# A two-layer graph kernel: block sums transposed by VectorE instead of TensorE, blocks of 480 columns, the input loaded between pieces of the adjacency

## The chip, the core and the metric

The kernel runs on one core of a Trainium2 chip. The metric is the device time of the whole program in microseconds (us), the median of several executions; lower is better. Engines are named as in the profile: PE is TensorE (matrix products), PEld its weight loads, DVE is VectorE, ACT is ScalarE, POOL is GpSimd, SP is SyncE, which here only issues DMA transfers.

## The reference

The inputs are `x` (3327 x 128) and a 0/1 matrix `adj` (3327 x 3327), all in fp32. Two layers follow each other, each of the form x + layer(relu(layernorm(x))):

```
# layer 0
h   = relu(layernorm(x))
deg = adj.sum(axis=1);  deg = 1 where deg == 0
agg = adj.T @ h / deg
y   = agg @ W_n.T + b_n + h @ W_c.T + b_c
x   = x + relu(batchnorm(y) * gamma + beta)
# layer 1: n = 3327, d = 128, h = 8
z = relu(layernorm(x))
q, k, v = (z @ W.T).reshape(128, n, 8)          # for Wq, Wk, Wv
a = einsum('dnh,dmh->dnm', q, k) / sqrt(128) + adj + adj
out = einsum('dnm,dmh->dnh', softmax(a, axis=2), v)
x = x + out.reshape(n, 1024) @ Wo.T
```

Nearly all the work is in the second layer: for each of 128 slices d, a 3327 x 3327 matrix of scores with an inner dimension of only 8, its exponential, and a product with v, which has 8 columns.

## The kernel before

**Layer 0.** The rows of the adjacency come in 26 chunks of 128 rows (tile `a`, 1.66 MB each, three buffers, issued by SP at L431). For each chunk, PE makes seven products (L433) that add up adj.T @ h in seven PSUM banks, ACT sums the rows (L437), and DVE takes a maximum (L440). PE needs `A` = relu(layernorm(x)) for that. In the kernel before, `x` is loaded into `xs` by two large and two small DMAs issued from ACT (L326, L328), and after them ACT issues the ten loads of weights and vectors (L331 to L337). Then seven rounds of `stats` (DVE statistics, ACT square root) and `normalise` (two small DVE operations, four ACT activations) make all of `A`, before the loop over chunks is recorded. `beside` puts transposes and small products of the same layer between chunks.

**Layer 1.** 32 groups (`NG`) of four slices d (`G`) follow each other. In a group the 3328 padded query columns are cut into seven blocks of `QB` columns (before: six of 476 and one of 472), and each block takes 13 steps (`SU`), in each of which two chunks of 128 keys are used. So there are 224 blocks and 2912 steps. The order of all engines is written by hand (manual schedule), in this one loop:

- `product` (L750): two products on PE give scores `s` of 128 keys x 2 x w queries in PSUM (three buffers, two banks each). There are four products in a step.
- For two or three of the four (`plain`), DVE adds the adjacency (`add`, L862) and writes to `d`; one step later a single ACT instruction takes the exponential of all of `d` (`late`, L907).
- For the others (`rest`; one in a step, two in the steps 3, 7 and 11, named `DOUBLE`), ACT takes the exponential straight from PSUM (L871), and POOL multiplies by weights exp(2 adj) that were stored earlier (L874, tile `wt`).
- `second` (L623): PE multiplies the exponentials by v and adds up over the 13 steps, three steps behind (`LAG`). The result of a block, in one bank `av`, holds for each of the four slices (partitions 32b to 32b+8) nine rows: eight sums and the sum that divides them. Two banks `av` alternate between blocks.
- `finish` divides a finished block and stores it. It is a generator; `step()` runs it on, one part each time, in the steps of the next block that `PARTS` lists (step 7 is served at another place of the loop, after the first `add`). In the kernel before the parts are: step 3, DVE copies `av` to `avs` in SBUF (L633); steps 5 and 6, two products each with the identity on PE (L640), which write the transposed sums back into `av`, with the query columns on partitions; step 7, three DVE operations (L648 to L651) divide; step 8, SP issues one DMA to `att` (L658; at the end of a group a second small one, L665).
- `begin` and `go_on` put parts of the next group's projections (L208) and of the last group's output product (L269, L279) into steps 7, 8, 11 and 12; they use the bank `av` of the block that has just been finished.
- `fetch` issues the loads of `at` (adjacency, L738, four buffers) and `wt` (L734, three buffers) two steps ahead, on SP. The loads of the next group's q, k and v are spread over the steps, and POOL sorts k (L192).

The function `attention_shifted` is for other inputs and isn't run here; it calls `finish` too.

Of the kernel before, what the change touches and what calls it, by code (L numbers as in the profile page):

```python
# [9 lines left out]
F32 = mybir.dt.float32  # L10
F32R = mybir.dt.float32r
I32 = mybir.dt.int32
AF = mybir.ActivationFunctionType
ALU = mybir.AluOpType
# [4 lines left out]
N = 3327  # L19
D = 128  # L20
H = 8
P = 128
NC = 26
T = N * D
NP = NC * P
NB = 512
QB = 476
G = 4
EPS = 1e-5
HALF = 0.5 / math.sqrt(D)  # L30
# [3 lines left out]
CH = 4 * NP // D  # L34
NG = D // G
DOUBLE = (3, 7, 11)
PARTS = (3, 5, 6, 7, 8)

def pieces(r):

    return [(p0, p1) for p0, p1 in ((0, r // 16 * 16), (r // 16 * 16, r)) if p1 > p0]
# [3 lines left out]
def tile_two_layer_gnn(  # L47
# [17 lines left out]
    nc = tc.nc  # L65
# [5 lines left out]

    qblocks = [(n0, min(QB, NP - n0)) for n0 in range(0, NP, QB)]

# [13 lines left out]
    att = dram.tile([TP, H], F32, name="att")  # L87
# [8 lines left out]
    attb = att[:T].rearrange("(d n) h -> d n h", n=N)  # L96
    atr = att.rearrange("(n u) h -> n (u h)", u=D)

    ident = const.tile([P, P], F32, name="ident")
# [8 lines left out]
    eps = const.tile([P, 1], F32, name="eps")  # L108
    nc.vector.memset(eps, EPS)
    wqk = [const.tile([P, H * D], F32, name=n) for n in ("wq", "wk", "wv")]  # L110
    wo = const.tile([P, H, D], F32, name="wo")
# [189 lines left out]
    with tc.tile_pool(name="l0", bufs=1) as l0, tc.tile_pool(  # L301
        name="l0adj", bufs=3
    ) as ap, tc.tile_pool(name="l0s", bufs=2) as sp, tc.tile_pool(
        name="l0last", bufs=1
# [3 lines left out]
        xs = ll.tile([P, NC, D], F32, name="xs")  # L308
        A = l0.tile([P, NC, D], F32, name="A")
# [6 lines left out]
        wn = l0.tile([P, D], F32, name="wn")  # L316
        wc = l0.tile([P, D], F32, name="wc")
        cols = l0.tile([P, 4], F32, name="cols")
        bias = l0.tile([P, 1], F32, name="bias")
# [2 lines left out]

        xr = x[: (NC - 1) * P, :].rearrange("(c p) d -> p c d", p=P)
        nc.vector.memset(xs[:, NC - 1, :], 0.0)
        for c0, c1 in ((0, 8), (8, NC - 1)):
            nc.scalar.dma_start(xs[:, c0:c1, :], xr[:, c0:c1, :])  # L326
        for p0, p1 in pieces(N - (NC - 1) * P):
            nc.scalar.dma_start(  # L328
                xs[p0:p1, NC - 1, :], x[(NC - 1) * P + p0 : (NC - 1) * P + p1, :]
            )  # L330
        nc.scalar.dma_start(wc, WcT)  # L331
        for i, b in enumerate((b_n, b_c, gamma, beta)):
            nc.scalar.dma_start(cols[:, i : i + 1], b.rearrange("o d -> d o"))
        nc.scalar.dma_start(wn, WnT)
        for t, w in zip(wqk, (WqT, WkT, WvT)):
            nc.scalar.dma_start(t, w)
        nc.scalar.dma_start(wo, WoT.rearrange("(e p) o -> p e o", p=P))  # L337

        st = l0.tile([P, NC, 6], F32, name="ln_st")
        mv = l0.tile([P, NC, 2], F32, name="ln_mv")  # L340
# [4 lines left out]
        def stats(i, root=True):  # L345
            cs = range(4 * i, min(NC, 4 * i + 4))
            for c in cs:
                nc.vector.bn_stats(st[:, c, :], xs[:, c, :])
            for c in cs:
                nc.vector.bn_aggr(mv[:, c, :], st[:, c, :])  # L350
            if root:
                roots(4 * i, min(NC, 4 * i + 4))

        def roots(c0, c1):
            nc.scalar.activation(sd[:, c0:c1], mv[:, c0:c1, 1], AF.Sqrt, bias=eps)
# [7 lines left out]
        def normalise(i, dst):  # L363

            factors(4 * i, min(NC, 4 * i + 4))
            for c in range(4 * i, min(NC, 4 * i + 4)):
                nc.scalar.activation(  # L367
                    dst[:, c, :], xs[:, c, :], AF.Relu,
                    bias=mr[:, c : c + 1], scale=rs[:, c : c + 1],
                )  # L370
# [7 lines left out]
            return pt[:, :n, :], slice(4 * i, 4 * i + n)  # L378

        NQ = (NC + 3) // 4  # L380
        stats(0)
        for i in range(NQ):
            if i + 1 < NQ:
                stats(i + 1)
            normalise(i, A)
        nc.vector.tensor_add(bias, cols[:, 0:1], cols[:, 1:2])

        def beside(x):

            if x < NQ:  # L390
                pt, cs = turned(x, A, aside)
                nc.scalar.copy(B[:, cs, :], pt)
            elif x < 2 * NQ:
                n0 = (x - NQ) * NB
                w = min(NB, NP - n0)
                nc.tensor.matmul(
                    aside[:, :w], wc, B2[:, n0 : n0 + w], start=True, stop=True
                )
                nc.scalar.activation(
                    C2[:, n0 : n0 + w], aside[:, :w], AF.Identity, bias=bias  # L400
                )
            elif x < 2 * NQ + 4:
                i = x - 2 * NQ
                sq = sp.tile([P, NB], F32, name="sq")
                w = wqk[i // 2][:, i % 2 * NB : (i % 2 + 1) * NB]
                nc.gpsimd.tensor_tensor(sq, w, w, ALU.mult)  # L406
                nc.tensor.matmul(aside[:1, :], ones[:, :1], sq, start=True, stop=True)  # L407
                nc.vector.tensor_reduce(norm[:, i : i + 1], aside[:1, :], AX.X, ALU.max)
# [20 lines left out]
        for c in range(NC):  # L429
            a = ap.tile([P, 7 * NB], F32, name="a")  # L430
            nc.sync.dma_start(a[:, :N], adj[c * P : (c + 1) * P, :])  # L431
            for i, (n0, w) in enumerate(blocks):
                nc.tensor.matmul(  # L433
                    acc[i][:, :w], A[:, c, :], a[:, n0 : n0 + w],
                    start=(c == 0), stop=(c == NC - 1),
                )
            nc.scalar.activation(  # L437
                junk, a[:, :N], AF.Copy, accum_out=deg[:, c : c + 1]
            )
            nc.vector.tensor_reduce(  # L440
                amax[:, c : c + 1], a[:, :N], AX.X, ALU.max, apply_absolute_value=True
            )
            if c >= 1:
                beside(c - 1)

            i = c - 2 * NQ - 5
            if 0 <= i < NQ - 2 and 4 * i + 4 <= c:
                spread(i)
# [17 lines left out]
        b = l0.tile([1, 6], F32, name="bound")  # L466
# [118 lines left out]
        q, k, v = sets[0]  # L585
# [41 lines left out]

    def finish(rp, av, d0, n0, w):

        J = 4  # L630
        R = -(-w // J)
        avs = rp.tile([P, QB], F32, name="avs")
        nc.vector.tensor_copy(avs[:, : R * J], av[:, : R * J])  # L633
        yield

        pt = av[:, : J * G * (H + 1)].rearrange("p (j q) -> p j q", j=J)

        some = ident.rearrange("p (b h) -> p b h", h=32)[:, :, : H + 1]
        for j in range(J):
            nc.tensor.matmul(  # L640
                pt[:R, j, :], avs[:, j : j + (R - 1) * J + 1 : J], some, start=True, stop=True
            )
            if j % 2:
                yield
        pv = pt.rearrange("p j (b h) -> p b j h", h=H + 1)
        ri = rp.tile([P, G, J], F32, name="ri")

        nc.vector.tensor_scalar(ri[:R], pv[:R, :, :, H], 1e-30, None, ALU.max)  # L648
        nc.vector.reciprocal(ri[:R], ri[:R])
        o = rp.tile([P, G, J, H], F32, name="oq")  # L650
        nc.vector.tensor_tensor(  # L651
            o[:R], pv[:R, :, :, :H], ri[:R].unsqueeze(3).to_broadcast([R, G, J, H]),
            ALU.mult,
        )
        yield

        r, j = divmod(min(w, N - n0), J)
        nc.sync.dma_start(  # L658
            attb[bass.ds(d0, G), n0 : n0 + r * J, :].rearrange(
                "b (p j) h -> p b (j h)", j=J  # L660
            ),
            o[:r].rearrange("p b j h -> p b (j h)"),
        )
        if j:
            nc.sync.dma_start(  # L665
                attb[bass.ds(d0, G), n0 + r * J : n0 + r * J + j, :].rearrange(
                    "b (o j) h -> o b (j h)", o=1
                ),
                o[r : r + 1, :, :j, :].rearrange("p b j h -> p b (j h)"),
            )  # L670

    def rows_of(c):
        return min(P, N - c * P)

    def attention():


        with tc.tile_pool(name="adj", bufs=4) as ap, tc.tile_pool(
# [13 lines left out]
            if True:  # L692
# [35 lines left out]
                def fetch(x):  # L728
                    while wanted and wanted[0][0] <= x:
                        _, kind, i, y, c = wanted.pop(0)  # L730
                        n0, w = qblocks[y]
                        if kind:
                            a = wp.tile([P, QB], F32, name="wt")
                            nc.sync.dma_start(a[:, :w], wd[c - WC, :, n0 : n0 + w])  # L734
                        else:
                            a = ap.tile([P, 2, QB], F32, name="at")
                            n = min(2, WC - 2 * c)
# [25 lines left out]
                def more_weights(i, y, s):  # L763
# [13 lines left out]
                    if phase == 0:  # L777
                        have["w"] = wk.tile([P, 2, QB], F32, name="t4")
                        nc.sync.dma_start(
# [59 lines left out]
                for x, (i, y, s) in enumerate(steps):  # L839
# [15 lines left out]
                    plain, rest = pairs(s)  # L855
                    d = ep.tile([P, 3, 2, QB], F32, name="d")
                    es = [d[:, j] for j in range(len(plain))]
# [36 lines left out]
                    else:  # L894
                        add(2, product(i, y, *plain[2]))
                    if s in PARTS and s != DOUBLE[1]:
                        step()
# [219 lines left out]
```

## Time and profile before

| what | value |
|---|---|
| median of 3 runs | 10377.37 us (10372.69 to 10381.02) |
| the profiled execution: its time, its span | 10381.98 us, 10380.2 us |
| mean granted TensorE clock in it | 0.992 |
| busy: PE, ACT, DVE, POOL | 9995.3, 9923.2, 9366.9, 8439.0 us |
| layer 0, until the first scores | 0 to 261.7 us |
| layer 1 | the rest, some 10100 us |
| L862, DVE add of 128 x 952 | 1.14 us |
| L871, ACT exponential of 128 x 952; L907, of 128 x 2856 | 0.97 us; 2.6 us |
| L633, DVE copy of a block's sums | 0.65 us, 224 times |
| L640, PE products with the identity | four entries of one part: 1.06 us, 448 parts |

Durations of single instructions run until their results are written, and instructions of one engine overlap at their ends, so that ten of them in a row take less than ten durations. A matmul of fp32 has two entries in the trace. "Idle before" is the time in which an engine had nothing running ahead of an instruction, with what ended that wait.

### The profile page before, as it was taken

What the parts mean: (1) busy time and instruction counts of PE and PEld (TensorE: products, weight loads), DVE (VectorE), ACT (ScalarE), POOL (GpSimd) and SP (SyncE); (2) the same over time, 40 slices, a digit from 0 to 9 for tenths busy, and PEclk for the clock granted to TensorE, in tenths of its full rate; (3) what the DMA queues carried; (4) which work ended last, traced back from release to release, by engine and by line L of the source; (5) the groups of instructions that cost most, each with busy time, mean ns of one, the idle gap of its engine ahead of it and who ended that gap; (6) DMA issues with size and microseconds to landing.
All of it is one profiled execution on the core that took longest, in us unless ns stands there. A gap on an engine that the chain in (4) does not pass through costs nothing. (4 is left out here: it accounts for less than half of the span.)

```text
span 10380.2 us, 189900 instructions
## 1 busy us (share of the span) xinstructions
PE 9995.3 (96%) x73327; PEld 3082.3 (30%) x73327; DVE 9366.9 (90%) x9533; ACT 9923.2 (96%) x6655; POOL 8439.0 (81%) x4317
## 2 busy tenths in 40 slices
PE   7899999999999999999999999999999999999999
PEld 3222222222222222222222222222222222222222
DVE  5789999999999999999999999999999999999998
ACT  4899999999999999999999999999999999999998
POOL 1678888888888888888888888888888888888887
PEclk9899999999999999999999999999999999999999
DMA  6766666666666666666665666666666665666554
GB/s 228 221 177 164 163 170 167 166 165 165 163 166 170 165 165 162 164 168 167 167 164 159 168 167 168 167 161 162 167 169 167 167 161 159 171 169 167 157 153 127
DMA packets 1114449, 1735.99 MB, mean 167 GB/s; under 512 B 194622, under 2 KB 1089980, under 8 KB 1105852
## 3 DMA queue, kind: packets, MB, share of 16 engines
q1 hardware_dynamic: 1108766, 1716.94, 60.9%
q8 instruction: 575, 9.42, 0.4%
q10 hardware_dynamic: 4350, 4.20, 0.1%
q14 instruction: 342, 2.80, 0.1%
q0 software_dynamic: 416, 2.63, 0.1%
HBM read 1621.05 MB, written 102.38 MB: 166 GB/s over the span
## 5 line engine op out<-in xcount | busy, mean ns | idle before, releaser
L862 DVE SCALAR_TENSOR_TENSOR d<-at,s 128x952 f32<-128x952 f32 x8064 | 8797.4, 1141 | 681.7 <-PE s L750 397.6
L874 POOL TENSOR_TENSOR f<-f,wt 128x952 f32<-128x952 f32 (+1 forms) x3584 | 7939.0, 2233 | 1674.3 <-ACT f L871 1649.9
L907 ACT ACTIVATE d<-d 128x2856 f32<-128x2856 f32 (+1 forms) x2912 | 7027.9, 2413 | 2.2 <-DVE d L862 1.9
L623 PE MATMUL av<-d,v 128*9 128x476 f32 x32256 | 5065.6, 566 | 0.7 <-ACT d L907 0.7
L750 PE MATMUL s<-q,k 32*128 32x476 f32 x23296 | 4087.3, 475 | 313.8 <-ACT f L871 243.5
L871 ACT ACTIVATE f<-s 128x952 f32<-128x952 f32 (+1 forms) x3584 | 3396.9, 970 | 281.8 <-PE s L750 266.0
L750 PEld LDWEIGHTS s<-q,k 32*128 32x128 f32 x23296 | 1739.5, 182 | 5500.2 <-DVE d L862 3005.9
L623 PE MATMUL av<-f,v 128*9 128x476 f32 x14336 | 2849.0, 566 | 0.0
L623 PEld LDWEIGHTS av<-d,v 128*9 128x9 f32 x32256 | 583.3, 88 | 1161.5 <-issue 1149.6
L640 PE MATMUL av<-ident,avs 128*119 128x36 f32 (+1 forms) x1792 | 474.1, 391 | 0.8 <-DVE avs L633 0.8
L640 PEld LDWEIGHTS av<-ident,avs 128*119 128x119 f32 (+1 forms) x1792 | 422.9, 308 | 103.1 <-issue 101.5
L623 PEld LDWEIGHTS av<-f,v 128*9 128x9 f32 x14336 | 316.6, 88 | 112.4 <-issue 88.7
L192 POOL CAST k<-ks 128x256 fp32r<-128x256 f32 x434 | 283.8, 654 | 0.0
L433 PE MATMUL acc<-a,A 128*128 128x512 f32 (+1 forms) x364 | 151.6, 569 | 24.2 <-ACT A L367 23.4
L238 POOL TENSOR_TENSOR o<-pf,o 104x512 fp32r<-104x512 f32 x124 | 160.0, 1291 | 9.9
L633 DVE COPY avs<-av 128x476 f32<-128x476 f32 (+1 forms) x224 | 145.4, 649 | 4.6 <-PE av L623 4.6
L440 DVE TENSOR_REDUCE amax<-a 128x1 f32<-128x3327 f32 x26 | 93.7, 3611 | 36.4 <-DMA a<-in_adj 36.4
L433 PEld LDWEIGHTS acc<-a,A 128*128 128x128 f32 x364 | 69.0, 192 | 109.0 <-issue 84.5
L236 DVE TENSOR_SCALAR pf<-av,low_half 104x512 f32<-104x512 f32 x62 | 46.6, 751 | 46.8 <-PE av L208 46.6
L406 POOL TENSOR_TENSOR sq<-wk 128x512 f32<-128x512 f32 x2 | 2.1, 1042 | 102.5 <-PE aside L407 102.5
L234 DVE COPY pf<-av 104x512 f32<-104x512 f32 x62 | 42.9, 692 | 46.9 <-PE av L208 46.9
L437 ACT ACTIVATE junk<-a 128x3327 bf16<-128x3327 f32 x26 | 77.5, 2979 | 7.1 <-DMA a<-in_adj 6.8
(123 smaller groups left out, 1032.3 us busy)
## 6 DMA issues: line engine op xcount, KB each, us to landing
at<-in_adjT SPq DMA_DIRECT2D x1728, 476.0 KB
wt<-wd SPq DMA_DIRECT2D x1536, 238.0 KB
at<-in_adjT SPq DMA_DIRECT2D x288, 472.0 KB
wt<-wd SPq DMA_DIRECT2D x256, 236.0 KB
ks<-kT SPq DMA_DIRECT2D x496, 104.0 KB
q<-qT SPq DMA_DIRECT2D x496, 104.0 KB
a<-in_adj SPq DMA_DIRECT2D x26, 1663.5 KB
kT<-o SPq DMA_DIRECT2D x128, 208.0 KB
```

Source lines behind the costliest of these rows:

```text
L192: nc.gpsimd.tensor_copy(k[:, c : c + n, half * 64 : half * 64 + 64], ks.bitcast(F32).rearrange("g (p c) -> g c p", c=NC)[:, c : c + n, :],)
L238: nc.gpsimd.tensor_tensor(o[:CH, 1], f[:CH], o[:CH, 0].bitcast(F32), ALU.subtract)
L433: nc.tensor.matmul(acc[i][:, :w], A[:, c, :], a[:, n0 : n0 + w], start=(c == 0), stop=(c == NC - 1),)
L440: nc.vector.tensor_reduce(amax[:, c : c + 1], a[:, :N], AX.X, ALU.max, apply_absolute_value=True)
L623: nc.tensor.matmul(av[32 * b : 32 * b + H + 1, :w], tiles[2][:, b, c, :], e, start=first, stop=last,)
L633: nc.vector.tensor_copy(avs[:, : R * J], av[:, : R * J])
L640: nc.tensor.matmul(pt[:R, j, :], avs[:, j : j + (R - 1) * J + 1 : J], some, start=True, stop=True)
L750: nc.tensor.matmul(p[:, x, :we], k[rs, c, :], q[rs, n0 : n0 + we], start=True, stop=True,)
L862: nc.vector.scalar_tensor_tensor(d[:, j, :, :w], have[0, i, y, c // 2][:, c % 2, :w] .unsqueeze(1).to_broadcast([P, 2, w]), SAFE / 2, p[:, ...
L871: nc.scalar.activation(f[:, :, :w], p[:, :, :w], AF.Exp, scale=2.0)
L874: nc.gpsimd.tensor_tensor(f[:, :, :w], f[:, :, :w], have[1, i, y, c][:, :w].unsqueeze(1).to_broadcast([P, 2, w]), ALU.mult,)
L907: nc.scalar.activation(flat, flat, AF.Exp, scale=2.0)
```

## The change

There are three edits.

1. `finish` no longer uses PE. DVE transposes the block's sums in squares of 32 x 32 (`nc.vector.transpose`), from `av` in PSUM to `avs` in SBUF. The columns of `av` are read with a stride of J (15, in the last block 14), so that a partition gets J neighbouring queries. The division then reads SBUF. The result goes out in four DMAs of 32 partitions, one for each slice (in the last block of a group eight, as the last query is padding). The parts now stand in steps 3, 7 and 8.
2. Blocks have 480 columns instead of 476: six of 480 and one of 448. All are multiples of 32. There are still seven blocks in a group.
3. `x` is loaded by SP, its first four chunks ahead of the adjacency, the rest behind its first and second chunk. `stats` and `normalise` run inside the loop over chunks. Weights and vectors are loaded by POOL instead of ACT. A first square root of a constant is put ahead on ACT.

```diff
-QB = 476
+QB = 480
-PARTS = (3, 5, 6, 7, 8)
+PARTS = (3, 7, 8)
...
-        for c0, c1 in ((0, 8), (8, NC - 1)):
-            nc.scalar.dma_start(xs[:, c0:c1, :], xr[:, c0:c1, :])
...
+        nc.sync.dma_start(xs[:, :4, :], xr[:, :4, :])
+        def load_x(c):
+            if c < 2:
+                c0, c1 = ((4, 12), (12, NC - 1))[c]
+                nc.sync.dma_start(xs[:, c0:c1, :], xr[:, c0:c1, :])
...
+        root = l0.tile([P, 1], F32, name="root")
+        nc.scalar.activation(root, eps, AF.Sqrt)
+        for t, w in zip(wqk, (WqT, WkT, WvT)):
+            nc.gpsimd.dma_start(t, w)
+        nc.gpsimd.dma_start(wc, WcT)
...
-        stats(0)
-        for i in range(NQ):
-            if i + 1 < NQ:
-                stats(i + 1)
-            normalise(i, A)
...
             nc.sync.dma_start(a[:, :N], adj[c * P : (c + 1) * P, :])
+            load_x(c)
+            if c < NQ:
+                if c == 0:
+                    stats(c)
+                normalise(c, A)
+                if c + 1 < NQ:
+                    stats(c + 1)
...
     def finish(rp, av, d0, n0, w):
-        J = 4
-        R = -(-w // J)
-        avs = rp.tile([P, QB], F32, name="avs")
-        nc.vector.tensor_copy(avs[:, : R * J], av[:, : R * J])
+        J = -(-w // 32)
+        avs = rp.tile([P, QB // 32, 32], F32, name="avs")
+        nc.vector.transpose(
+            avs[:, :J, :].rearrange("p j h -> p (j h)"),
+            av[:, : 32 * J].rearrange("p (q j) -> p j q", j=J),
+        )
         yield
-        pt = av[:, : J * G * (H + 1)].rearrange("p (j q) -> p j q", j=J)
-        some = ident.rearrange("p (b h) -> p b h", h=32)[:, :, : H + 1]
-        for j in range(J):
-            nc.tensor.matmul(
-                pt[:R, j, :], avs[:, j : j + (R - 1) * J + 1 : J], some, start=True, stop=True
-            )
-            if j % 2:
-                yield
...
+        nc.vector.tensor_scalar(ri[:, :J], avs[:, :J, H], 1e-30, None, ALU.max)
+        nc.vector.reciprocal(ri[:, :J], ri[:, :J])
...
+        r = 32 - (n0 + 32 * J > N)
+        for b in range(G):
...
+            nc.sync.dma_start(ab[:r], ob[:r])
+            if r < 32:
+                nc.sync.dma_start(ab[r:, : (J - 1) * H], ob[r:, : (J - 1) * H])
```

## The prediction

> **What bounds the kernel now.** I read the page's busy shares first, then the stretch table, to see whether the share is even over the run.
>
> ```profile
> PE 9995.3 (96%) x73327; PEld 3082.3 (30%) x73327; DVE 9366.9 (90%) x9533; ACT 9923.2 (96%) x6655; POOL 8439.0 (81%) x4317
> ...
> 2000.00:4000.00 2000.00, 1948.57 (x14557) 596.04 (x14553) 1841.95 (x1856) 1951.31 (x1298) 1680.73 (x855) 1.00 0.62 166
> ```
>
> The columns of the second line are the stretch, its length, busy time of PE, PEld, DVE, ACT and POOL, granted clock, DMA share and GB/s. PE and ACT both look full (97.5%), but the timelines tell them apart. First ACT over three steps of a block, then PE over the same time; the bracket is the idle time before an instruction and what ended it.
>
> ```profile
> 5005.22 2.64 ACT L907 ACTIVATE d<-d 128x2832 f32<-128x2832 f32 x1
> 5008.48 0.96 ACT L871 ACTIVATE f<-s 128x944 f32<-128x944 f32 x1 [0.62 <-PE s L750]
> 5009.33 2.56 ACT L907 ACTIVATE d<-d 128x2832 f32<-128x2832 f32 x1
> 5012.37 0.96 ACT L871 ACTIVATE f<-s 128x944 f32<-128x944 f32 x1 [0.48 <-PE s L750]
> ```
>
> ```profile
> 5005.58 0.49 PE L750 MATMUL s<-q,k 32*128 32x472 f32 x4
> 5005.99 1.06 PE L640 MATMUL av<-ident,avs 128*119 128x36 f32 x4
> 5006.99 0.57 PE L623 MATMUL av<-d,v 128*9 128x472 f32 x2
> ...
> 5009.90 1.06 PE L640 MATMUL av<-ident,avs 128*119 128x36 f32 x4
> ```
>
> ACT works without a hole except behind the two L640 parts, which keep PE from the next scores. In the 400 us from 4600 on, all ACT's waits are such pairs (0.59 to 0.62 and 0.47 to 0.49 us), one pair a block; blocks start 44.74 us apart (4606.19 to 4650.93). From 5015.7 on, steps without L640 follow at 3.29 to 3.35 us with ACT never idle. So ACT sets the pace, and L640 costs it 1.1 us a block. The groups of 1000 to 9000 us confirm the sum:
>
> ```profile
> L871 ACT ACTIVATE f<-s 128x952 f32<-128x952 f32 (+1 forms) x2863 | 2712.4, 970 | 193.8 <-PE s L750 181.3 <-POOL k L192 12.5
> L907 ACT ACTIVATE d<-d 128x2856 f32<-128x2856 f32 (+3 forms) x2327 | 5615.7, 2413 | 0.2
> ```
>
> 193.8 us over 179.5 blocks is 1.08 us a block. (The share put down to POOL's sorting is one member of a pair, at 4833.53 us with 0.48 us, so it is the same wait under another name.)
>
> **The change part by part.** *L640 leaves.* ACT's 1.08 us a block, times 224 blocks, is 242 us. Counting L640's own busy time (474 us) would be too much: part of it is time that PE has to spare, as between 5015 and 5019 PE itself waits. Nothing above 242 us is to be had in steady state, since ACT is then full. The first group runs at a granted clock of 0.77 to 1.00 with ACT only 77 to 97% busy (300 to 660 us), where the delays may be longer; at most another 1 us for each of its 7 blocks, kept for the range.
>
> *The transpose takes the copy's place on DVE, in step 3.* The trace has no such instruction. The nearest row is the copy it replaces: same engine, same source in PSUM, 128 x 476 in 0.65 us. The far rows, by pace per element: POOL's product, 2.23 us for 952, would give 1.13 us for 480; DVE's reciprocal, slowest of all, takes 0.25 us for 16 elements against 0.17 for the scaling of the same 16, so 5.3 ns more for each, on the copy's 1.35 ns: 3.2 us. Below the copy's 0.65 us I see no reason for it to fall, since it reads as many elements. I take 0.7 us. What hides it: step 3 has only two adds, 2 x 1.09 us (13 adds in a row take 14.22 us), in a step of some 3.36 us, so 1.18 us are free; a step of three adds leaves 0.09. Up to about 1.2 us the transpose costs nothing; each further us goes into ACT's wait. Queued behind it on DVE are the adds of step 4, on which L907 and the score buffers wait.
>
> *The division in step 7* keeps its three operations (0.17 + 0.25 + 0.29 us) and reads about as many elements, 15, 15 and 120 instead of 16, 16 and 128. It frees the bank `av` no longer, the transpose does that four steps earlier: PE's waits on L651 before the projections (72.6 us over the run) go, but as ACT shows no wait there, I count nothing. DVE, 920 us busy in 1000, has 41.1 us in a block and keeps a block of 43.7 us to 94%.
>
> *Four DMAs on SP instead of one, in step 8*: 3 x 0.33 us more, with the wait for L651 in front of them as now. Behind them stands the next `at`. In the trace that one is issued at 5014.65 and is for the step two further on than the engines' next, some 7 us ahead, and lands in 3.5 us. Hidden; if not, 1 us a block. The packets fall from 476 of 128 B to 128 of 480 B.
>
> *Blocks of 480.* Columns, instructions and steps stay as many as before: nothing. *The end*: 1.9 us of L640 at 10358.8 go, three to seven more issues of 0.33 us come: nothing.
>
> *Layer 0.* PE's first product waits until 23.45 us, because ACT stands in two small loads:
>
> ```profile
> 2.31 12.04 ACTq L328 DMA_DIRECT2D xs<-in_x  x2
> ...
> 20.86 1.28 ACT L355 ACT_TABLE_LOAD   x1 [19.46 <-DMA cols<-in_beta]
> ```
>
> Now 256 KB of `x` lead SP's queue. With 155 GB/s up to 4 us and 428 after, they are in at about 4 us; statistics, root, factors and one activation (0.9 + 0.4 + 0.3 + 0.35 + 0.4) make the first `A` at 6.5; the first chunk lands at about 8. Then data rules: up to the third chunk 6.6 MB, with POOL's 2.2 MB of weights at 0.4 MB per us they take until some 24 us, and the fourth chunk starts at 24 + 6.6 = 30.6 us. Before, it started near 43.2. From there PE sets the pace as before (seven products of two entries in some 6 us; inside the loop ACT has about 5.6 us and DVE 5.2 a chunk, both less). Gain: 12 us; bounds 16 (the start at 8) and 0 (all lost again to loads).
>
> *Sum*: 10381.98 - 242 - 12 = 10128 us for an execution like the profiled one, which is 4.6 us above the median. On the median: **10123 us**.
>
> **A rule against it.** Row first: the granted clock is 1.00 in all stretches from 1000 to 10000 us, and in steps without L640 too (1.00 in 5019.00 to 5022.30 and 5022.30 to 5025.65). The Trainium skill ("TensorE: Matmul & The Clock Gate", Part 1) says that the array falls to half its clock after an idle window of some 3.4 us, which speaks against taking work from PE. By the rule a block without L640 would be in danger only if PE paused that long; the trace's waits of PE in these steps are under 0.7 us, so both give the same sum here.
>
> The same skill ("VectorE: DVE Perf Modes", The three transpose paths) has 311 ns for 128 columns on VectorE; my estimate from it, 3.75 times as much, is 1.17 us for 480, and the sum would still be as above. No run here shows it yet.
>
> **The rivals.** *Half the gain comes back (a second wait).* DVE goes to 94% and POOL to 86%; the adds or POOL's products are then late in some steps. For it: DVE already makes PE wait for L862 often. Against it: steps 7 and 11, where DVE has the division, a projection copy of 0.69 to 0.75 us and a wait of 0.6 to 0.85 us on top, show no ACT idle. Price: 121 us back, 10244 us.
>
> *DVE's transpose is slow (slower than before).* It is one instruction, in step 3 of each block. At 3.2 us, the reciprocal's pace, 3.2 - 1.27 (free in steps 3 and 4) = 1.93 us a block are new and 1.08 gone: 224 x 0.85 = 190 more, less 12: 10555 us. It decides from 1.27 + 1.08 + 0.05 (layer 0's 12 us over 224) = 2.4 us on. For it: nothing in the trace moves data across partitions on DVE. Against it: it would have to be 3.7 times the copy.
>
> *Layer 0 loses instead of winning.* The rest of `x` and the weights come ahead of the third chunk; at no gain 10135 us, well inside the forecast. *The change doesn't act*: the instructions of L640 are gone from PE's order, so this is left out.
>
> **How the numbers follow.** Forecast 80% (10095 to 10160: group 0's 7 us, layer 0's 4, the scatter of 10 below; layer 0's 12, SP's 224 x 0.1 above). Half back 10%, with anything between 10160 and 10350. Slow transpose 7%, most of it above 10377. About no change 3%. The range 10095 to 10240 takes in the forecast and half of the second case. Over 0.2% (21 us, about what a measurement of this kernel can tell from no change) faster: 0.90; within: 0.02; slower: 0.08.
>
> **What would show it.** Right: L871's idle before it falls from 194 to under 30 us in 8000, ACT is over 99% busy, blocks stand 44.0 us apart (480 columns: 43.66 x 480/476), the transpose's mean is under 1.2 us, the first L433 starts at 7 to 10 us. Wrong: a transpose over 1.3 us with L871 or L907 waiting on L862 in steps 4 to 6; waits of similar length elsewhere in the block; or waits on `at`.

## The result and the profile after

| | kernel before | changed kernel |
|---|---|---|
| median | 10375.32 us (4 runs, 10372.69 to 10381.02) | 10683.61 us (4 runs, 10676.46 to 10692.11) |
| ratio | | 1.0297, 95% interval 1.0279 to 1.0315 |
| mean granted TensorE clock in the profile | 0.992 | 0.960 |

The change makes the kernel 3% slower; 10123 us were forecast. Lines in the changed kernel's profile that answer to those shown of before: the busy line of the page, one stretch (stretch, length, busy time of PE, PEld, DVE, ACT and POOL, granted clock, DMA share, GB/s), and groups of 1000 to 9000 us.

```profile
PE 9998.2 (94%) x71535; PEld 2758.6 (26%) x71535; DVE 9693.6 (91%) x9533; ACT 9938.1 (93%) x6655; POOL 8452.5 (79%) x4327
```

```profile
2000.00:4000.00 2000.00, 1891.96 (x13760) 515.45 (x13758) 1851.78 (x1800) 1895.59 (x1259) 1636.02 (x834) 0.97 0.60 161
```

```profile
L907 ACT ACTIVATE d<-d 128x2880 f32<-128x2880 f32 (+3 forms) x2257 | 5460.8, 2419 | 136.2 <-DVE d L862 136.2
...
L871 ACT ACTIVATE f<-s 128x960 f32<-128x960 f32 (+1 forms) x2778 | 2650.0, 981 | 279.3 <-PE s L750 273.3 <-POOL f L874 5.9
...
L653 DVE TENSOR_SCALAR ri<-avs 128x15 f32<-128x15 f32 (+1 forms) x173 | 335.1, 1937 | 0.0
```

ACT now idles 415.5 us in these 8000, 2.4 us in each of 174 blocks; before it was 1.08. The third line names the cause: the scaling that starts the division, 15 elements in each partition, takes 1.94 us in the mean. Its counterpart before took 0.17 us each time, for 16 elements from PSUM:

```profile
L648 DVE TENSOR_SCALAR ri<-av 119x16 f32<-119x16 f32 (+1 forms) x179 | 30.0, 168 | 0.0
```

The transpose itself, L646, takes 0.67 us, as forecast.

The timeline of one block's step 7 shows what holds it (start, duration, instruction, idle time before it):

```profile
5047.99 2.24 POOL L874 TENSOR_TENSOR f<-f,wt 128x960 f32<-128x960 f32 x1 [1.10 <-ACT f L871]
5048.30 1.96 DVE L653 TENSOR_SCALAR ri<-avs 128x15 f32<-128x15 f32 x1
...
5050.29 0.25 DVE L654 RECIPROCAL ri<-ri 128x15 f32<-128x15 f32 x1
...
5050.58 0.28 DVE L656 TENSOR_TENSOR oq<-avs,ri 128x120 f32<-128x120 f32 x1
5050.78 1.15 DVE L862 SCALAR_TENSOR_TENSOR d<-at,s 128x960 f32<-128x960 f32 x1
...
5051.98 0.48 PE L750 MATMUL s<-q,k 32*128 32x480 f32 x2 [1.14 <-DVE d L862]
```

L653 ends at 5050.26, POOL's product at 5050.23. Over the run its duration lies between 0.17 us (first block) and 2.20 us, close to one whole product of POOL. In 222 of the 224 blocks it starts while a product of POOL runs, and ends 0.03 to 0.06 us after that product; in the other two it takes 0.17 and 0.18 us. Behind it, in DVE's order, stands the second add of step 7; PE waits 1.14 us for the score buffer that this add frees, and ACT then waits 0.55 us for scores and 0.81 us for the late `d`. This is a mild block. In the block before PE's pause was 1.71 us, and then this happened (PE's pause, ACT, then the stretches):

```profile
5004.04 0.48 PE L750 MATMUL s<-q,k 32*128 32x480 f32 x2 [1.71 <-DVE d L862]
```

```profile
5006.72 0.97 ACT L871 ACTIVATE f<-s 128x960 f32<-128x960 f32 x1 [0.83 <-PE s L750]
5008.49 2.60 ACT L907 ACTIVATE d<-d 128x2880 f32<-128x2880 f32 x1 [0.79 <-DVE d L862]
5013.29 0.97 ACT L871 ACTIVATE f<-s 128x960 f32<-128x960 f32 x1 [2.20 <-PE s L750]
```

```profile
5006.00:5009.00 3.00, 3.00 (x20) 0.59 (x20) 2.22 (x2) 1.48 (x2) 3.00 (x2) 0.50 0.77 217
5009.00:5012.00 3.00, 3.00 (x18) 0.51 (x20) 1.66 (x2) 2.09 (x1) 1.39 (x1) 0.50 1.03 189
```

The granted clock is 0.50 (by the clock's records from 5005.43 to 5012.25 us), eight entries of L636 take 1.79 us instead of 0.99, and ACT loses 3.8 us in this block instead of 1.4.

### The profile page after: what moved, and what is told of

Same layout as the page of the kernel before. It is cut to its first block, busy times and chain, and to the rows that moved or that the text cites. A ratio compares the mean times of both kernels' runs of the same rounds, so it can differ in the third digit from the quotient of the medians.

```text
span 10682.1 us, 187244 instructions
## 1 busy us (share of the span) xinstructions
PE 9998.2 (94%) x71535; PEld 2758.6 (26%) x71535; DVE 9693.6 (91%) x9533; ACT 9938.1 (93%) x6655; POOL 8452.5 (79%) x4327
## 5 line engine op out<-in xcount | busy, mean ns | idle before, releaser
L874 POOL TENSOR_TENSOR f<-f,wt 128x960 f32<-128x960 f32 (+1 forms) x3584 | 7951.2, 2236 | 1974.9 <-ACT f L871 1943.5
L862 DVE SCALAR_TENSOR_TENSOR d<-at,s 128x960 f32<-128x960 f32 x8064 | 8739.5, 1140 | 711.6 <-PE s L750 580.6
L907 ACT ACTIVATE d<-d 128x2880 f32<-128x2880 f32 (+1 forms) x2912 | 7043.2, 2419 | 173.3 <-DVE d L862 173.3
L636 PE MATMUL av<-d,v 128*9 128x480 f32 x32256 | 5275.1, 586 | 0.8 <-ACT d L907 0.8
L750 PE MATMUL s<-q,k 32*128 32x480 f32 x23296 | 4326.3, 488 | 616.6 <-DVE d L862 375.4
L871 ACT ACTIVATE f<-s 128x960 f32<-128x960 f32 (+1 forms) x3584 | 3419.4, 980 | 404.7 <-PE s L750 396.4
L750 PEld LDWEIGHTS s<-q,k 32*128 32x128 f32 x23296 | 1836.8, 186 | 6097.8 <-DVE d L862 4121.1
L636 PE MATMUL av<-f,v 128*9 128x480 f32 x14336 | 2966.1, 583 | 0.0
L636 PEld LDWEIGHTS av<-d,v 128*9 128x9 f32 x32256 | 585.7, 89 | 1248.7 <-issue 1246.3
L653 DVE TENSOR_SCALAR ri<-avs 128x15 f32<-128x15 f32 (+1 forms) x224 | 427.0, 1906 | 0.0
L636 PEld LDWEIGHTS av<-f,v 128*9 128x9 f32 x14336 | 317.9, 89 | 154.0 <-issue 141.6
L646 DVE STREAM_TRANSPOSE avs<-av 128x480 f32<-128x480 f32 (+1 forms) x224 | 150.7, 673 | 4.3 <-PE av L636 4.3
```

The costliest lines, as they stand in the source:

```text
L636: nc.tensor.matmul(av[32 * b : 32 * b + H + 1, :w], tiles[2][:, b, c, :], e, start=first, stop=last,)
L646: nc.vector.transpose(avs[:, :J, :].rearrange("p j h -> p (j h)"), av[:, : 32 * J].rearrange("p (q j) -> p j q", j=J),)
L653: nc.vector.tensor_scalar(ri[:, :J], avs[:, :J, H], 1e-30, None, ALU.max)
L750: nc.tensor.matmul(p[:, x, :we], k[rs, c, :], q[rs, n0 : n0 + we], start=True, stop=True,)
L862: nc.vector.scalar_tensor_tensor(d[:, j, :, :w], have[0, i, y, c // 2][:, c % 2, :w] .unsqueeze(1).to_broadcast([P, 2, w]), SAFE / 2, p[:, ...
L871: nc.scalar.activation(f[:, :, :w], p[:, :, :w], AF.Exp, scale=2.0)
```

## The experiments

The theory: some DVE instructions with both sides in SBUF wait until the POOL instruction running beside them has ended. Rivals: reading the transposed sums with a stride of 32 elements is slow in itself; or whatever reads first after the transpose has to wait. The kernel before ran beside each set of runs, with medians of 10374 to 10378 us.

**1. Without the scaling.**

```diff
-        nc.vector.tensor_scalar(ri[:, :J], avs[:, :J, H], 1e-30, None, ALU.max)
-        nc.vector.reciprocal(ri[:, :J], ri[:, :J])
+        nc.vector.reciprocal(ri[:, :J], avs[:, :J, H])
```

> The changed kernel with the division's first operation (L653, the scaling that keeps the divisor above 1e-30) left out, so that the reciprocal reads the transposed sums directly. Theory (port): L653 stands for 1.9 us because it reads and writes SBUF only, in a form that must wait until the POOL product running beside it has ended. Without it, either the wait is gone (reciprocal 0.25 us, the product with it 0.28 us, run at about 10130 us), or it moves to the next operation, the product of two SBUF operands, which then takes 1.2 to 2.2 us (run near 10600 us). Rival (stride): reading the transposed sums with a stride of 32 elements is slow in itself; then the reciprocal takes 1.9 us and the run stays at about 10680 us. Rival (fresh data): whatever reads first after the transpose waits; the same signs as the stride.

Measured: 10522.55 us (one run). The timeline of its step 7:

```profile
5021.52 2.24 POOL L873 TENSOR_TENSOR f<-f,wt 128x960 f32<-128x960 f32 x1 [0.62 <-ACT f L870]
5021.84 0.24 DVE L653 RECIPROCAL ri<-avs 128x15 f32<-128x15 f32 x1
...
5022.11 1.79 DVE L655 TENSOR_TENSOR oq<-avs,ri 128x120 f32<-128x120 f32 x1
```

Both rivals fall here: the reciprocal reads the strided, fresh sums, beside a running product of POOL, in 0.24 us. The wait has moved to the next operation, the product of two operands in SBUF (mean 1.77 us in 1000 to 9000 us). In the changed kernel that operation (0.28 us) had only come after L653 had already waited. So two kinds of DVE instruction wait, and the reciprocal isn't one of them. The run is 77 us below the 10600 forecast for this case.

**2. POOL's product of step 7 in two halves**, DVE as in the change.

```diff
+                        if s == DOUBLE[1]:
+                            for h in range(2):
+                                nc.gpsimd.tensor_tensor(
+                                    f[:, h, :w], f[:, h, :w], have[1, i, y, c][:, :w], ALU.mult,
+                                )
```

> The changed kernel, DVE untouched; only POOL's products of step 7 are issued as two halves of 128 x 480 each. Theory (port): L653 waits for the end of one POOL instruction, so its mean falls from 1.91 us to between 0.6 and 1.1 us, and the run to about 10450 us (10350 to 10550). Rivals (stride, fresh data): L653 stays at 1.9 us and the run at 10680 us or above.

```profile
5007.89 2.37 POOL L876 TENSOR_TENSOR f<-f,wt 128x480 f32<-128x480 f32 x2 [0.61 <-ACT f L871]
5008.21 0.93 DVE L653 TENSOR_SCALAR ri<-avs 128x15 f32<-128x15 f32 x1
...
5009.17 0.25 DVE L654 RECIPROCAL ri<-ri 128x15 f32<-128x15 f32 x1
...
5009.46 0.94 DVE L656 TENSOR_TENSOR oq<-avs,ri 128x120 f32<-128x120 f32 x1
```

L653 falls to 0.92 us, as the theory said: the wait is as long as what is left of one POOL instruction. The time, 10517.23 us (one run), lies within 10350 to 10550 us but 67 us above the 10450 named, probably because L656 now meets the second half and takes 0.94 us.

**3. The kernel before, with one such instruction more.**

```diff
+        scratch = rp.tile([P, 15], F32, name="scratch")
+        nc.vector.tensor_scalar(scratch, ones[:, :15], 1e-30, None, ALU.max)
         nc.vector.tensor_scalar(ri[:R], pv[:R, :, :, H], 1e-30, None, ALU.max)
```

> The kernel before, all of it, plus one DVE scaling of 128 x 15 from a constant tile in SBUF to a scratch tile in SBUF, in step 7 ahead of the division. Theory (port): that one instruction takes about 1.9 us in the mean, though nothing is transposed, nothing strided and nothing fresh is read, and the run goes from 10375 to 10600 us or more (PE is late in step 7 as in the changed kernel). Rivals (stride, fresh data): it takes 0.1 to 0.2 us and the run stays below 10420 us.

Measured: 11008.02 us (one run), 630 us more than before, for an instruction that takes 0.16 us where POOL is idle. Its group, of 1000 to 9000 us:

```profile
L648 DVE TENSOR_SCALAR scratch<-ones 128x15 f32<-128x15 f32 x168 | 366.9, 2184 | 0.0
```

Nothing is transposed, strided or fresh there. The cause doesn't need the transpose.

**4. Transposed within PSUM, divided from PSUM.**

```diff
-        nc.vector.transpose(
-            avs[:, :J, :].rearrange("p j h -> p (j h)"),
-            av[:, : 32 * J].rearrange("p (q j) -> p j q", j=J),
-        )
+        square = av[:, : 32 * J].rearrange("p (q j) -> p j q", j=J)
+        nc.vector.transpose(square, square)
         yield
+        avs = av[:, : 32 * J].rearrange("p (h j) -> p h j", j=J)
```

> The changed kernel, but the transpose writes back into the same places of PSUM, and the division reads its values from there, as in the kernel before; everything else is as in the change. Theory (port): no operation of the division has SBUF alone on both sides any more except the reciprocal, which did not wait in the kernel before; L653 is back at 0.17 us, ACT's waits behind the removed products on PE are gone, and the run takes 10130 us (10110 to 10170), as the prediction had it. Rivals (stride, fresh data): the scaling still takes over 1 us and the run stays above 10500 us.

Measured: 10083.58 us (4 runs), ratio to before 0.9715 (0.9699 to 0.9731). The scaling takes 0.16 us again, and ACT has no hole left:

```profile
L651 DVE TENSOR_SCALAR ri<-av 128x15 f32<-128x15 f32 (+1 forms) x185 | 30.3, 164 | 0.0
```

```profile
2000.00:4000.00 2000.00, 1947.39 (x14636) 540.57 (x14636) 1883.42 (x1909) 2000.00 (x1339) 1731.95 (x880) 1.00 0.63 169
```

So the wait of the division in SBUF is the whole difference between 10684 and 10084 us: 600 us, or 2.7 us a block. The gain is larger than forecast, which run 9 takes up.

**5. The waiting operations on POOL itself.** The scaling goes to POOL in step 5, the product to POOL in step 7; DVE keeps the reciprocal; the transpose goes to SBUF as in the change.

```diff
-PARTS = (3, 7, 8)
+PARTS = (3, 5, 7, 8)
-        nc.vector.tensor_scalar(ri[:, :J], avs[:, :J, H], 1e-30, None, ALU.max)
+        nc.gpsimd.tensor_scalar(ri[:, :J], avs[:, :J, H], 1e-30, None, ALU.max)
+        yield
...
-        nc.vector.tensor_tensor(
+        nc.gpsimd.tensor_tensor(
```

> The changed kernel with the two operations of the division that meet POOL moved to POOL itself: the scaling in step 5, the product with the reciprocals in step 7; DVE keeps only the reciprocal. The transpose still goes to SBUF. Theory (port, two forms of DVE instruction that wait for POOL): no DVE instruction is left that waits, ACT has no idle, the run is near the one that divides from PSUM, 10083 to 10120 us. Rival (any DVE access to SBUF alone beside POOL may wait; the reciprocal was only lucky to come after one that had waited): the reciprocal shows over 1 us and the run stays above 10400 us.

Measured: 10081.21 us (4 runs), 0.9715 (0.9699 to 0.9731). The reciprocal never took more than 0.25 us in 224 blocks, so the rival falls. Both ways out are worth the same.

**6. PE kept busy during the wait.** L653 waits as in the change; the two extra products on PE compute nothing that is used.

```diff
                     add(1, product(i, y, *plain[1]))
+                    if s == DOUBLE[1] and ending:
+                        for n in (NB, P):
+                            nc.tensor.matmul(
+                                avs2[(i * len(qblocks) + y + 1) % 2][:, :n], ident,
+                                wqk[0][:, :n], start=True, stop=True,
+                            )
```

> The changed kernel, with the wait of L653 left as it is, plus two products on PE (128 x 512 and 128 x 128, results unused) in step 7 of each block, at the place where PE stands still for 1.1 to 1.7 us. Theory (port and clock): a part of the loss is PE's clock, which falls to 0.5 in blocks whose pause is long; filled, the granted clock goes from 0.96 to over 0.985, ACT's idle from 2.4 us a block to about 1.5, and the run falls to some 10470 us though PE has more to do. Rival (the clock only follows, the loss is all DVE's wait): the run stays at 10680 us or gets longer.

Measured: 10430.00 us (one run), mean granted clock 0.992, ACT's idle 237.3 us in 8000 (1.3 us in each of 178 blocks), L653 still 1.95 us in the median. More work on PE made the kernel 254 us faster, 40 us more than the forecast for this case. PE's pauses, which in the changed kernel were 1.1 to 2.2 us long, are at most 0.85 us here, and the clock stays at 1.00:

```profile
2000.00:4000.00 2000.00, 1945.17 (x14280) 557.38 (x14278) 1892.94 (x1845) 1940.47 (x1289) 1674.23 (x851) 1.00 0.60 165
```

By this one run, about 250 of the 600 us go through the clock, which falls when PE pauses, and some 350 are DVE's delay itself. What the two products cost PE was not measured apart, so the clock's part may be larger.

**7. Layer 0's edit alone**, and **8. blocks of 480 alone** (only `QB = 480` in the kernel before).

> Only the third edit of the change: the loads of x between the adjacency's chunks, weights from POOL; finish, the steps and blocks of 476 as in the kernel before. By the first scores on PE, which stand at 253.82 us in the changed kernel and at 261.67 us in the one before, this edit is worth 7.9 us: 10367 to 10370 us. The prediction had 12 us, 10363. Were layer 0's edit a part of the loss, the run would be above 10377 us.

> The kernel before with only the blocks changed: six of 480 columns and one of 448 instead of 476 and 472. As many columns, instructions and steps as before: no change, 10365 to 10390 us, and seven blocks in 312.9 us. Rival (the blocks of 480, with rows of adjacency that start on multiples of 1920 B, are a part of what the version that divides from PSUM gains beyond the forecast): seven blocks in 311.5 us or less, the run at 10330 us or less.

Layer 0's edit: 10371.09 us (10 runs) against 10377.81, ratio 0.9994 (0.9984 to 1.0003). The blocks: 10381.05 us (10 runs) against 10374.15, ratio 1.0006 (0.9996 to 1.0015), seven blocks in 313.0 us. Neither can be told from nothing, so neither explains the loss of 308 us, and the blocks don't explain the extra gain.

**9. The products of L640 alone.** The four matmuls are left out of the kernel before (the division then works on untransposed sums and its divisor is kept above 1).

> The kernel before with only the four products of L640 left out (the division then works on untransposed sums, with a divisor of at least 1); blocks of 476, layer 0 and the steps as before. It measures alone what these products cost. By ACT's idle time in the trace, 1.08 us a block, the run falls by 242 us to 10135 us and seven blocks take 305.3 us. Other reading: instructions of ACT overlap by some 0.12 us when they follow without a wait, and each of the two waits in a block also loses that overlap, so that a block loses 1.32 us; then seven blocks take 303.7 us and the run 10082 us.

Measured: 10081.71 us (4 runs) against 10374.15, ratio 0.9715 (0.9699 to 0.9731), seven blocks in 303.7 us instead of 312.9. That is 292 us or 1.31 us a block. The second reading holds: 1.08 us of visible idle time, and for each of the two waits some 0.12 us of overlap that is lost as well.

**10. Layer 0 once more**: the version of run 4, with weights and vectors loaded by SP behind the fifth chunk.

```diff
+            if c == 4:
+                load_w()
```

> The version that divides from PSUM, with one more change in layer 0: weights and vectors are loaded by SP behind the fifth chunk of the adjacency instead of by POOL at the start. If layer 0's gain was 8 us and not 12 because 2.2 MB of weights delay the second chunk (PE waits 7.45 us for it until 23.45 us), that wait falls below 2 us, the first scores come at about 247 us instead of 254, and the run is 5 to 8 us shorter than the version without this, 10076 to 10080 us. If the loads of x are what delays it, nothing changes.

The early part came as expected: no wait for the second chunk, first scores at 247.41 us. The time didn't follow: 10088.37 us (4 runs) against 10083.58. PE meets a 2.03 us wait for a chunk at 43.3 us instead. In the profiled executions this version is 6.8 us ahead at mid-run (a block's transpose at 4940.04 against 4946.82 us), 2.5 us at the last division (10059.1 against 10061.6 us) and 3.0 us in span (10080.3 against 10083.3 us), while the medians differ by 5 us the other way. It can't be told from nothing, and where the early gain goes was not settled. First scores also differ by 3.5 us between kernels with the same layer 0 (261.67 and 258.13 us), so that effects of this size can't be followed here.

## Why the prediction was wrong, point by point

**The step that failed** is the division. The prediction said that it "keeps its three operations" and "reads about as many elements", and counted nothing; the scaling that it priced at 0.17 us took 1.94. What changed was the memory, not the number of elements: before, the scaling and the product read PSUM; after, they read SBUF, while POOL is 79% busy with products in SBUF. Runs 1 to 5 show this wait moved to the next operation, halved, added to the kernel before, and taken away in two ways. Step 7 has two adds like step 3, but the division and a projection's copy stand there already, and the next add is queued behind; no run put such a wait into another step.

The rule was to be had beforehand. The Trainium skill ("SBUF — State Buffer", SBUF: two separate sides) says that VectorE and GpSimd share one pair of ports as an exclusive lock, held for a whole instruction, and that a VectorE instruction in a two-port mode, or with two SBUF inputs while GpSimd reads SBUF, blocks against it. The trace agrees for the product of two SBUF inputs (1.77 us in run 1). It agrees for the scaling (1.94 us) if that ran in a two-port mode, which no view here shows. The prediction looked for a rule against the change in TensorE's clock and stopped there.

**The clock.** The prediction set the rule aside, since PE's waits were under 0.7 us. With the new wait they weren't: a pause of 1.71 us was followed by a clock of 0.50 from 5005.43 to 5012.25 us, one of 1.14 us was not. The length alone doesn't decide. In 1000 to 9000 us of the changed kernel the clock fell to 0.50 after 27 of 99 pauses of 1.1 to 1.2 us, 17 of 25 of 1.7 us and 41 of 49 of 2.1 to 2.2 us. All 93 slow stretches there begin on one grid of 3.41 us and last one or two steps of it, and in the step ahead of each PE had stood idle for 1.07 to 2.22 us in all; in the other steps at full clock it was idle for at most 1.18 (in run 3, though, up to 1.63). So it also matters how a pause lies on that grid. The rule ("TensorE: Matmul & The Clock Gate", Part 1, in the Trainium skill) speaks of an idle window of some 3.4 us; here a pause half as long was enough, and the measurement decides. Run 6 puts a price on it, about 250 us.

**ACT sets the pace, and L640 costs it time**: right, by run 9, but mis-sized. The term was sized at 242 us and measured 292. The working added up "idle before", which counts from the end of the last instruction; ACT's instructions overlap at their ends when they follow without a wait, and a wait costs that overlap too.

**The transpose**: 0.7 us taken, 0.67 measured, hidden in step 3. The rival that it is slow falls; but its form, one DVE instruction of 2 to 3 us that delays the adds, came true for another instruction in another step. The row that the prediction took from the Trainium skill ("VectorE: DVE Perf Modes", The three transpose paths) is for bf16; the estimate of 1.17 us from it was above the 0.67 us measured here in fp32. **Four DMAs** instead of one: hidden, since ACT has no idle in run 4. **Half the gain comes back**: not in run 4, where ACT is busy throughout with DVE at 94%. **Blocks of 480**: nothing, as forecast. **Layer 0**: 12 us forecast, 7.9 by the first scores in the profile, 6.7 in the medians of run 7, whose interval takes in no change at all. The prediction let PE's fourth chunk start at 30.6 us. It started at 38.21 (in the kernel before at 44.00), because PE, done with the first chunk at 16.0 us, waited for the second until 23.45. With the weights loaded later (run 10) that wait is gone, and the fourth chunk starts at 29.09 us.

Without the failed step the sum would have been right in direction and the gain a little small: 10123 us against 10084 in run 4.

## What to carry to other kernels

When a change moves an operand between PSUM and SBUF, ask for each DVE instruction that touches it what POOL does at that moment: with POOL working on SBUF, a scaling of 15 elements or a product of two SBUF operands took as long as what was left of POOL's instruction, while reading from PSUM, or a reciprocal, did not wait. Look at the maximum of such an instruction, not at its element count, and at what is queued behind it. And price a wait of a pipelined engine as the idle time plus the overlap that it breaks (here 0.12 us on 0.54).

## What was not expected of the hardware

- One DVE instruction of 0.16 us, put beside POOL's products, cost 2.8 us a block, 630 us in all (run 3).
- Useless products on PE in its pauses of 1.1 to 2.2 us made the kernel 254 us faster, by holding the granted clock at 0.992 instead of 0.960 (run 6).
- The transpose in squares may write to the very places of PSUM that it reads: 0.68 us for 128 x 480 with a stride of 15 elements (run 4), the same as to SBUF.
